# Two residual layers on one core: how the group carries of a sorted prefix sum reach the gathered rows

## The chip, the cores and the metric

One core of a Trainium2 chip runs the whole program. The metric is the device time in microseconds of one execution; the median of a few executions is given. A profile of one execution, with every instruction and transfer, stands beside it.

## What is computed

For each of 32 batches `x[b]` is a 512 x 1024 matrix (channels by nodes), and there are two layers, each with a residual and a layer normalization over the 1024 nodes. Cut to what matters:

```python
def _L0_gnn_ref(x, wq, wk, wm, bm):
    q = jnp.einsum('c,bcn->bn', wq, x)
    k = jnp.einsum('c,bcn->bn', wk, x)
    scores = q[:, None, :] + k[:, :, None]
    scores = jnp.where(scores > 0, scores, NEG_SLOPE * scores)
    att = jax.nn.softmax(scores, axis=-1)
    agg = jnp.einsum('bcn,bmn->bcm', x, att)
    out = jnp.einsum('oc,bcm->bom', wm, agg) + bm[None, :, None]
    return jax.nn.relu(out)

def _L1_gnn_ref(x, support, kernel, bias):      # support = kernel = adj
    W = support * kernel
    return jnp.einsum('bnf,nm->bmf', x, W) + bias

x = _layernorm(x + _L0_gnn_ref(x, wq, wk, adj, bm), axis=-1)
x = _layernorm(x + _L1_gnn_ref(x, adj, adj, bias), axis=-1)
```

Everything is float32. Layer 0's attention has scores that are a sum of one number of the row and one of the column, through a leaky ReLU. So the kernel does not form the 1024 x 1024 matrix. It sorts the columns by `q`. For a row with key `k`, the columns above a threshold have weight exp(q+k) and those below it exp(0.01 (q+k)). Each row is then a mix of two sums over sorted columns: one over all ranks from one side, one over all ranks from the other, both cut at that row's rank.

## The kernel before

**The stages of a batch**, with the short names that the order of the work uses. `ld` loads x (2 MB, four buffers in the pool `xp`). `pa pc co cc ro rc` make q and k. `rk` (VectorE) counts each column's rank among q, `ct` (ScalarE) counts for each row how many q lie above its threshold; `re` and `ce` turn them into row numbers `to` and `of`. `z` (TensorE) multiplies x by adj in eight blocks of 128 nodes, `zc` (ScalarE) copies each block to `zt`, and `sc` (GpSimd) scatters its 128 rows of 514 numbers to `sorted_z` in DRAM, at the ranks. `sl` (SyncE) loads `sorted_z` back, so that partition p holds the eight ranks 8p to 8p+7.

**The sums.** `se` makes the two exponentials, `u` (VectorE) the running sums over the eight ranks of each partition from one side, `d` those from the other. A sum over whole partitions, the carry, is missing in each. `cu` and `cd` (TensorE) make it by a product with a triangular matrix (`before` or `behind`) from the partition's totals, `uc` and `dc` (ScalarE) copy it out of PSUM. Then VectorE adds the carry to all ranks of the partition: `tu` (two parts, L405), `td` (two parts, L405), and `te` (L414) for the last row. `tw` (two parts, L422, SyncE) writes the table, 1024 rows of 2 x 514 numbers, to DRAM, and `tl` (L425) its last row.

**The mix.** `g` (GpSimd, L432) gathers eight times 128 rows of the table to `got`, by `of`. `mw` makes weights for four of the eight parts, `ms` (ScalarE) and `mx` (VectorE) mix the two halves of each row, `t` (TensorE) transposes to PSUM, `r` (VectorE) adds the residual, `s0` (ScalarE) sums squares. Layer 0's root is taken in one step when all four parts of `s0` are done: `rt` (ScalarE, square root, L500) and `rce` (VectorE, reciprocal, L504). `n0` (ScalarE) scales.

**Layer 1.** One level of a Strassen-Winograd product: `t1` to `t4` on VectorE, `U V Z Y 11 12 21` on TensorE, copies and sums on ScalarE and VectorE, then `s1`, `r1` (GpSimd), `n`, and the store `st`. Its operands `T3` and `T4` stand in `zt`, the buffer that `zc` fills and `sc` reads.

**Buffers.** The tile `tab`, which receives the loaded ranks and holds both running sums until `tw` has read them, has one buffer, and so has `got`. `zt` is one buffer too. `sorted_z` and `table` have two each in DRAM.

**What sets the order.** The order is written out: three strings of words, `head`, `loop` and `tail`, are read word by word and each word issues one step for one batch. Every engine and every queue works off its own instructions strictly in that order. `loop` covers one batch's worth of all steps on five batches in different stages (in a word such as `g.-2.3` the first number is the batch, counted from the loop's base, the second the part). In the kernel before it runs for 14 bases after a head of 11 batches; the tail drains the rest. Since GpSimd's queue is in order too, a gather whose table has not landed holds up every scatter and root behind it.

Of the kernel before, what the change touches and what calls it, by code (L numbers as in the profile page):

```python
# [41 lines left out]
P = 128  # L43
# [6 lines left out]
def adj_resnorm_kernel(  # L50
# [49 lines left out]
    room = one.tile([P, NT, 2 * ZR], F32, tag="tab", name="bias_in")[0:6, :, 0:H]  # L100
    for h in range(2):
# [7 lines left out]
    before = const.tile([P, P], F32, name="before")  # L109
    nc.vector.memset(before, 1.0)  # L110
    nc.gpsimd.affine_select(
        before, before, pattern=[[1, P]], compare_op=ALU.is_gt, fill=0.0, base=0,
# [23 lines left out]
    zero = one.tile([P, ZR], F32, tag="carry", name="zero")[0:1, :]  # L136
    nc.vector.memset(zero, 0.0)
    sorted_z = [dr.tile([N, ZR], F32, name=f"sorted_z_{i}") for i in range(2)]
    table = [dr.tile([N + 1, 2 * ZR], F32, name=f"table_{i}") for i in range(2)]
    for t in table:  # L140
        nc.scalar.dma_start(out=t[N : N + 1, ZR:], in_=zero)
    spare = const.tile([1, 1], F32, name="spare")
# [145 lines left out]
    def count_end(b):  # L288
        s = st[b]
        s.of = s4.tile([P, NT], U32, tag="of", name=f"of_{b}")  # L290
        nc.vector.tensor_scalar(s.of, s.sign, 0.5, N / 2, ALU.mult, ALU.add)
        s.bd = s4.tile([P, 2, NT], F32, tag="bd", name=f"bd_{b}")
        nc.vector.tensor_scalar(s.bd[:, 0, :], s.k, s.top, 0.0, ALU.add, ALU.min)
        nc.vector.tensor_scalar(s.bd[:, 1, :], s.k, s.top, 0.0, ALU.add, ALU.max)
# [37 lines left out]
    def sums_load(b, h):  # L332


        s = st[b]
        if h == 0:
            apart(f"ranks {b}", s.scatters)
            s.tab = one.tile([P, NT, 2 * ZR], F32, tag="tab", name=f"tab_{b}")
            s.zs = s.tab[:, :, ZR : 2 * ZR]
            s.ac = sp.tile([P, 2, NT], F32, tag="ac", name=f"ac_{b}")  # L340
        rows = sorted_z[b % 2].rearrange("(p j) c -> p j c", j=NT)
        at = slice(h * NT // 2, (h + 1) * NT // 2)
        nc.sync.dma_start(out=s.zs[:, at, :], in_=rows[:, at, :])
# [30 lines left out]
    def carry(b, m, v):  # L374
# [3 lines left out]
        for h in range(2):  # L378
            t = p1.tile([P, C], F32, tag="m", name=f"carry_ps_{b}_{h}_{m is before}")[:, 0:half]
# [9 lines left out]
    def carry_up(b):  # L389
        st[b].cup = carry(b, before, st[b].end)  # L390

    def carry_up_copy(b):
        carry_copy(st[b].cup, st[b].tab[:, 0, 0:ZR])

    def carry_down(b):
        st[b].cdown = carry(b, behind, st[b].zs[:, 0, :])
# [5 lines left out]
    def spread_carry(v, c):  # L402
        n = v.shape[1]
        c = c[:, 0:D].rearrange("p (o c) -> p o c", o=1).broadcast_to([P, n, D])
        nc.vector.tensor_tensor(v, v, c, ALU.add)  # L405

    def table_up(b, h):
        lo, hi = ((1, 4), (4, 8))[h]
        spread_carry(st[b].tab[:, lo:hi, 0:D], st[b].tab[:, 0, 0:ZR])

    def table_up_end(b):

        s, on = st[b], slice(96, P)
        nc.vector.tensor_tensor(s.end[on, 0:D], s.end[on, 0:D], s.tab[on, 0, 0:D], ALU.add)  # L414

    def table_down(b, h):
        spread_carry(st[b].zs[:, 4 * h : 4 * h + 4, 0:D], st[b].carry)

    def table_write(b, h):
        rows = table[b % 2][0:N, :].rearrange("(p j) c -> p j c", j=NT)  # L420
        at = slice(4 * h, 4 * h + 4)
        nc.sync.dma_start(out=rows[:, at, :], in_=st[b].tab[:, at, :])  # L422

    def table_last(b):
        nc.sync.dma_start(out=table[b % 2][N : N + 1, 0:ZR], in_=st[b].end[P - 1 : P, :])  # L425


    def gather(b, j):
        s = st[b]
        if j == 0:  # L430
# [3 lines left out]
            in_offset=bass.IndirectOffsetOnAxis(ap=s.of[:, j : j + 1], axis=0),  # L434
        )
# [62 lines left out]
    def root0(b):  # L498
            v = st[b].v0
            nc.scalar.activation(v[1], v[1], AF.Sqrt, scale=1.0 / N**3, bias=eps)  # L500

    def root0_end(b):
            v = st[b].v0
            nc.vector.reciprocal(v[1], v[1])  # L504
    
# [129 lines left out]
    def store(b, m):  # L635
# [10 lines left out]
        "cd": carry_down, "dc": carry_down_copy, "tu": table_up, "te": table_up_end,  # L646
        "td": table_down, "tw": table_write, "tl": table_last, "g": gather, "mw": mix_weights,
        "ms": mix_scale, "mx": mix, "t": turn, "r": residual, "s0": spread0, "rt": root0, "rce": root0_end,
# [5 lines left out]
    pool_ops = ("sc", "g", "r1")  # L654
# [10 lines left out]
    bias.0 ld.1 ld.2 ld.3 z.0.0 z.0.1 pa.0 z.0.2 pc.0 zc.0.0 zc.0.1 co.0 zc.0.2 pa.1 cc.0 ro.0  # L665
    pc.1 z.0.3 rc.0 rk.0.0 ct.0.5 ct.0.2 rk.0.1 z.0.5 ct.0.3 rk.0.6 zc.0.3 rk.0.4 ct.0.7 z.0.4
    rk.0.5 ct.0.1 rk.0.7 rk.0.2 z.0.6 zc.0.4 zc.0.5 rk.0.3 ct.0.0 oq.0 re.0 sc.0.4 z.0.7 zc.0.6
    sc.0.1 ct.0.6 sc.0.5 ct.0.4 sc.0.3 co.1 zc.0.7 z.1.0 cc.1 sc.0.6 sc.0.2 sc.0.0 ro.1 z.1.6
    sc.0.7 rc.1 ce.0 ct.1.0 rk.1.1 zc.1.0 rk.1.3 z.1.2 zc.1.6 sl.0.0 ct.1.7 sl.0.1 oq.1 rk.1.0
    rk.1.2 z.1.1 zc.1.2 rk.1.7 ct.1.1 rk.1.4 we.0 rk.1.6 z.1.5 se.0.0 ct.1.6 u.0.0 u.0.1 ct.1.2  # L670
    u.0.2 se.0.1 pa.3 ct.1.5 u.0.3 u.0.4 ct.1.4 z.1.7 u.0.5 zc.1.5 ct.1.3 u.0.6 u.0.7 zc.1.1
    pc.3 rk.1.5 z.1.4 zc.1.7 d.0.7 d.0.6 ce.1 d.0.5 z.1.3 zc.1.4 re.1 d.0.4 sc.1.7 d.0.3 sc.1.0
    d.0.2 sc.1.5 co.3 d.0.1 zc.1.3 cu.0 cc.3 d.0.0 sc.1.3 ro.3 uc.0 cd.0 sc.1.6 te.0 tu.0.1 pa.2
    sc.1.1 sc.1.2 z.2.0 tu.0.0 pc.2 dc.0 sc.1.4 td.0.0 z.2.2 rc.3 tw.0.0 td.0.1 ct.3.3 ct.3.0
    co.2 z.2.5 rk.3.4 tw.0.1 zc.2.0 tl.0 we.1 rk.3.0 ct.3.7 zc.2.2 rk.3.3 z.2.3 zc.2.5 ct.3.4
    rk.3.6 ct.3.1 rk.3.1 ct.3.6 z.2.6 rk.3.7 zc.2.3 cc.2 ct.3.2 rk.3.2 sl.1.0 g.0.0 ct.3.5
    sl.1.1 rk.3.5 ro.2 g.0.1 zc.2.6 z.2.1 rc.2 g.0.2 rk.2.0 ct.2.7 g.0.3 ct.2.4 g.0.5 rk.2.3
    z.2.4 g.0.4 rk.2.2 se.1.0 ct.2.3 g.0.7 rk.2.1 z.2.7 g.0.6 zc.2.4 rk.2.7 zc.2.1 ce.3 re.3
    rk.2.4 se.1.1 z.3.0 rk.2.6 zc.2.7 ct.2.0 rk.2.5 ct.2.5 mw.0.0 z.3.1 u.1.0 ms.0.3 re.2 oq.2
    ms.0.0 u.1.1 sc.2.3 ms.0.1 u.1.2 ct.2.6 sc.2.5 mx.0.0 u.1.3 z.3.4 ms.0.2 sc.2.2 mx.0.3  # L680
    mw.0.1 sc.2.0 mx.0.2 ms.0.5 sc.2.6 mx.0.1 ms.0.6 z.3.2 mx.0.5 ms.0.7 sc.2.1 mx.0.6 ms.0.4
    mx.0.7 ct.2.2 sc.2.4 mx.0.4 u.1.4 sc.2.7 t.0.3 u.1.5 t.0.1 r.0.3 r.0.1 t.0.0 s0.0.3 u.1.6
    zc.3.4 t.0.2 zc.3.0 r.0.0 zc.3.1 z.3.5 s0.0.1 u.1.7 s0.0.0 r.0.2 d.1.7 s0.0.2 oq.3 cu.1
    d.1.6 sc.3.1 rt.0 d.1.5 d.1.4 zc.3.2 d.1.3 uc.1 z.3.3 sc.3.2 rce.0 zc.3.5 d.1.2 n0.0.0
    sc.3.0 d.1.1 n0.0.1 d.1.0 n0.0.2 tu.1.0 cd.1 zc.3.3 U.0.0 dc.1 t1.0 sc.3.3 n0.0.3 td.1.0
    11.0.0 td.1.1 tw.1.0 Z.0.0 11.0.1 tu.1.1 Zc.0.0 Uc.0.0 ct.2.1 U.0.1 t2.0 tw.1.1 te.1 V.0.0
    t3.0 tl.1 ce.2 12.0.0 Vc.0.0 Uc.0.1 V.0.1 up.0.0 Y.0.0 Vc.0.1 s1.0.0 sl.2.0 Z.0.1 lr.0.0
    we.2 sl.2.1 r1.0.0 t4.0 Y.0.1 Zc.0.1 g.1.0 12.0.1 lr.0.1 g.1.1 se.2.0 21.0.0 u.2.0 g.1.2
    u.2.1 g.1.3 21.0.1 u.2.2 up.0.1 se.2.1 g.1.7 ll.0.0 z.3.6 ld.4 u.2.3 s1.0.1 u.2.4 we.3
    r1.0.1 ls.0.0 u.2.5 s1.0.2 u.2.6 ll.0.1 u.2.7 r1.0.2 cu.2 d.2.7 ls.0.1 d.2.6 z.3.7 uc.2  # L690
    mw.1.0 zc.3.6 te.2 g.1.4 s1.0.3 d.2.5 sc.3.6 n.0.0 tu.2.1 pa.4 g.1.5 ms.1.3 ms.1.2 tu.2.0
    g.1.6 ms.1.1 z.4.5 pc.4 zc.3.7 sc.3.4 n.0.2 d.2.4 mx.1.1 sc.3.5 ms.1.0 d.2.3 n.0.1 sc.3.7
    mx.1.2 co.4 z.4.4 d.2.2 st.0.1 r1.0.3 mw.1.1 mx.1.0 ms.1.7 d.2.1 ms.1.5 cc.4 ms.1.6 d.2.0
    ro.4 zc.4.5 mx.1.5 ms.1.4 cd.2 mx.1.7 n.0.3 mx.1.4 z.4.0 zc.4.4 rc.4 st.0.3 dc.2 tl.2 st.0.0
    mx.1.6 st.0.2 ct.4.0 mx.1.3 td.2.0 ct.4.1 t.1.3 t.1.1 ct.4.5 r.1.3 z.4.1 tw.2.0 ct.4.4 r.1.1
    zc.4.0 td.2.1 s0.1.1 t.1.0 ct.4.2 t.1.2 r.1.0 tw.2.1 s0.1.3 z.4.6 oq.4 r.1.2 s0.1.0 rk.4.1
    ct.4.3 z.4.3 rk.4.2 s0.1.2 rk.4.0 zc.4.1 rt.1 z.4.7 g.2.0 sl.3.0 zc.4.3 rce.1 rk.4.7 sl.3.1
    n0.1.2 g.2.1 rk.4.6 n0.1.0 g.2.4 n0.1.1 rk.4.4 z.4.2 g.2.2 zc.4.6 rk.4.5 n0.1.3 g.2.3 t1.1
    ct.4.6 g.2.7 U.1.1 rk.4.3 zc.4.2 se.3.0 g.2.6 t2.1 11.1.1 g.2.5 Uc.1.1 u.3.0 ct.4.7 u.3.1
    U.1.0 re.4 u.3.2 sc.4.3 se.3.1 u.3.3 11.1.0 sc.4.0 ce.4 u.3.4 sc.4.1 V.1.1 mw.2.0 u.3.5  # L700
    ms.2.2 sc.4.2 ms.2.0 Z.1.0 mx.2.2 ms.2.3 sc.4.4 zc.4.7 mx.2.3 Vc.1.1 Z.1.1 u.3.6 ms.2.1
    Uc.1.0 mw.2.1 u.3.7 V.1.0 ms.2.6 mx.2.1 Zc.1.0 mx.2.6 12.1.0 Vc.1.0 d.3.7 ms.2.5 t3.1 ms.2.4
    cu.3 up.1.0 ms.2.7 Zc.1.1 Y.1.0 t4.1 s1.1.0 Y.1.1 mx.2.7 uc.3 r1.1.0 lr.1.0 mx.2.4 21.1.0
# [259 lines left out]
```

## Time and profile before

| | |
|---|---|
| median of 3 runs | 2069.77 us (2066.95 to 2071.07) |
| the profiled execution | 2069.97 us, of which the span from first to last instruction is 2068.1 us |
| mean granted TensorE clock | 0.989 |
| busy | TensorE 2005.4 us, VectorE 1686.9, ScalarE 1494.8, GpSimd 848.7 |
| moved by DMA | 541.04 MB, mean 262 GB/s |

A row of the groups gives line, engine, operation, output and input, count, then busy time and mean duration of one, then the idle time of the engine before it and what ended that idle time. A row of a table by windows gives the stretch, its length, then for TensorE, its weight loads, VectorE, ScalarE and GpSimd the busy microseconds with the number of instructions, then the granted clock, the mean busy share of the core's 16 DMA engines, and GB/s. Queue q0 carries GpSimd's transfers, q1 those of SyncE.

### The profile page before, as it was taken

To read this page: it belongs to the slowest core of one execution; us is meant where nothing else is said; L and a number is where in the kernel's file an instruction comes from. 1 tells how busy PE (TensorE), PEld (TensorE's weight loads), DVE (VectorE), ACT (ScalarE), POOL (GpSimd) and SP (SyncE) were. 2 spreads that over 40 slices of the span, in tenths; PEclk is the share of its full clock that TensorE was granted. 3 is DMA by queue.
4 is the path that set the end of the run, shared out by engine and by line. 5 is a ranking of instruction groups with operands and counts; after the bars stand their busy time and mean duration, and the time that the engine had idled before them with its cause. 6 is when DMAs were issued, how large, how long until landed. Compare 5 with 4: busy or idle time off the path is not lost.

```text
span 2068.1 us, 22068 instructions
## 1 busy us (share of the span) xinstructions
PE 2005.4 (97%) x6609; PEld 958.9 (46%) x6609; DVE 1686.9 (82%) x2778; ACT 1494.8 (72%) x2560; POOL 848.7 (41%) x1088
## 2 busy tenths in 40 slices
PE   8999999999999999999999999999999999999976
PEld 4444444444444444544444444444544444444432
DVE  5988888887788888888888888888888888788663
ACT  3567777776777777777787777787777787767666
POOL 4234443453443443443443443443443443444331
PEclk9999999999999999999999999999999999999988
DMA  5568767766677766677766677766677756677752
GB/s 224 199 241 324 286 231 285 311 231 237 247 301 294 291 245 270 246 286 295 296 245 269 246 285 295 287 256 264 250 281 296 301 212 272 240 295 271 275 204 81
DMA packets 137967, 541.04 MB, mean 262 GB/s; under 512 B 14404, under 2 KB 14416, under 8 KB 129656
## 3 DMA queue, kind: packets, MB, share of 16 engines
q1 hardware_dynamic: 80464, 337.47, 41.6%
q0 software_dynamic: 57344, 202.15, 25.3%
q8 instruction: 52, 0.85, 0.2%
q14 instruction: 67, 0.55, 0.1%
q10 hardware_dynamic: 40, 0.02, 0.0%
HBM read 270.29 MB, written 269.29 MB: 261 GB/s over the span
## 4 chain that ended last, share of the span: by engine, by line
PE 71%; DMA 7%; DVE 6%; POOL 3%; ACT 2%; issue 2%; SPq 0%; ACTq 0%; DVEq 0%; POOLq 0%
PE z_ps L310 30%; PE sum_ps L540 16%; PE pair_ps L540 8%; DMA got<-table,of 5%; PE agg_ps L482 5%; PE pair_ps L575 4%; POOL got L432 3%; PE qk_ps L221 2%; DMA table<-end 1%; DVE got L459 1%; PE carry_ps_False L380 1%; DVE tab L405 1%; PE q_tp L252 1%; PE carry_ps_True L380 1%; PE sum_ps L538 1%
## 5 line engine op out<-in xcount | busy, mean ns | idle before, releaser
L310 PE MATMUL z_ps<-adj_t,x 128*128 128x512 f32 x2048 | 908.7, 593 | 2.9 <-ACT zt L316 2.0
L310 PEld LDWEIGHTS z_ps<-adj_t,x 128*128 128x128 f32 x2048 | 382.8, 190 | 441.9 <-issue 430.6
L324 POOL DMA_INDIRECT sorted_z<-zt,to x256 | 327.0, 1277 | 423.7 <-ACT zt L316 323.1
L432 POOL DMA_INDIRECT got<-table,of x256 | 268.8, 1050 | 331.9 <-DVE junk_v L271 117.3
L271 DVE SCALAR_TENSOR_TENSOR junk_v<-qb,qkc,tie 128x1024 uint8<-128x1024 f32 x256 | 328.5, 1283 | 6.0
L284 ACT ACTIVATE junk_s<-qb,qkc 128x1024 bf16<-128x1024 f32 x256 | 294.2, 1149 | 28.8 <-DVE qb L261 20.5
L475 POOL TENSOR_SCALAR var<-var 128x1 f32<-128x1 f32 x128 | 63.4, 496 | 427.0 <-ACT junk L468 411.8
L454 ACT ACTIVATE got<-got,w 128x512 f32<-128x512 f32 x256 | 170.5, 716 | 80.7 <-DVE w L449 61.1
L459 DVE SCALAR_TENSOR_TENSOR got<-got,w 128x512 f32<-128x512 f32 x256 | 185.2, 748 | 40.6 <-ACT got L454 39.2
L316 ACT COPY zt<-z_ps 128x512 f32<-128x512 f32 x256 | 145.5, 580 | 82.5 <-PE z_ps L310 82.2
L490 DVE SCALAR_TENSOR_TENSOR x<-agg_ps,nbm,x 128x1024 f32<-128x1024 f32 x128 | 160.4, 1281 | 17.6 <-PE agg_ps L482 17.4
L372 DVE SCALAR_TENSOR_TENSOR tab<-tab,ac 128x513 f32<-128x513 f32 x224 | 168.7, 753 | 2.7
L405 DVE TENSOR_TENSOR tab<-tab,carry 128x2052 f32<-128x2052 f32 x64 | 146.3, 2291 | 20.7 <-ACT carry L387 20.7
L631 ACT ACTIVATE g<-g,nb,var 128x1024 f32<-128x1024 f32 x128 | 157.6, 1233 | 6.0 <-POOL nb L625 6.0
L468 ACT ACTIVATE junk<-g,tot 128x1024 bf16<-128x1024 f32 x128 | 146.5, 1145 | 19.6 <-DVE g L595 11.9
L468 ACT ACTIVATE junk<-x,tot 128x1024 bf16<-128x1024 f32 x128 | 146.8, 1147 | 18.9 <-DVE x L490 18.0
L540 PE MATMUL sum_ps<-x,adj 128*128 128x512 f32 x256 | 132.7, 642 | 18.9 <-ACT x L508 18.9
L362 DVE SCALAR_TENSOR_TENSOR tab<-tab,ac 128x514 f32<-128x514 f32 x192 | 144.6, 753 | 4.4 <-ACT ac L348 0.9
L482 PE MATMUL agg_ps<-ident,got 128*128 128x128 f32 x1024 | 131.2, 280 | 16.0 <-DVE got L459 8.3
L508 ACT ACTIVATE x<-x,var 128x1024 f32<-128x1024 f32 x128 | 138.3, 1146 | 1.4 <-DVE var L504 1.3
L482 PEld LDWEIGHTS agg_ps<-ident,got 128*128 128x128 f32 x1024 | 116.5, 144 | 48.6 <-issue 17.1
L405 DVE TENSOR_TENSOR tab<-tab 128x1539 f32<-128x1539 f32 (+1 forms) x64 | 129.4, 2025 | 0.8 <-ACT tab L387 0.7
(121 smaller groups left out, 2614.2 us busy)
## 6 DMA issues: line engine op xcount, KB each, us to landing
table<-tab SPq DMA_DIRECT2D x64, 2056.0 KB
tab<-sorted_z SPq DMA_DIRECT2D x64, 1028.0 KB
x<-in_x_dram SPq DMA_DIRECT2D x128, 512.0 KB
out_dram<-g SPq DMA_DIRECT2D x128, 512.0 KB
sorted_z<-zt,to POOLq DMA_INDIRECT x256
got<-table,of POOLq DMA_INDIRECT x256
adj_in<-in_adj_dram SPq DMA_DIRECT2D x1, 1024.0 KB
table<-end SPq DMA_DIRECT2D x32, 2.0 KB
```

The costliest lines, as they stand in the source:

```text
L271: nc.vector.scalar_tensor_tensor(junk, s.qb, s.q[:, j : j + 1], tie[:, at : at + N], ALU.subtract, ALU.is_gt, accum_out=s.rank[:, j : j + 1],)
L284: nc.scalar.activation(junk, s.qb, AF.Sign, bias=s.k[:, j : j + 1], accum_out=s.sign[:, j : j + 1])
L310: nc.tensor.matmul(s.z[j], xt[:, c, j * P : (j + 1) * P], adj_t[:, c, :], start=(c == 0), stop=(c == CT - 1),)
L324: nc.gpsimd.indirect_dma_start(out=sorted_z[b % 2][:, :], out_offset=bass.IndirectOffsetOnAxis(ap=s.to[:, j : j + 1], axis=0), in_=zt[:, j ...
L372: nc.vector.scalar_tensor_tensor(v, v, c, s.zs[:, j + 1, 0:D], ALU.mult, ALU.add)
L405: nc.vector.tensor_tensor(v, v, c, ALU.add)
L432: nc.gpsimd.indirect_dma_start(out=s.got[:, j, :], out_offset=None, in_=table[b % 2][:, :], in_offset=bass.IndirectOffsetOnAxis(ap=s.of[:, ...
L454: nc.scalar.activation(down, down, AF.Copy, scale=s.w[:, 1, j : j + 1])
L459: nc.vector.scalar_tensor_tensor(up, up, s.w[:, 0, j : j + 1], down, ALU.mult, ALU.add)
L468: nc.scalar.activation(junk, t, AF.Square, bias=v[0][:, i : i + 1], scale=-float(N), accum_out=v[1][:, i : i + 1],)
L482: nc.tensor.transpose(s.agg[o][:, j * P : (j + 1) * P], s.got[:, j, o * P : (o + 1) * P], ident)
L540: nc.tensor.matmul(ps, a[:, k, g * P : (g + 1) * P], v[:, k, :], start=False, stop=(k == 1), skip_group_check=first is None,)
```

## The change

The additions `tu`, `td`, `te` and the write `tl` are gone. The table is written with the sums inside each partition alone. The carries go to a small table in DRAM of their own (`carries`, 129 rows of 2 x 514 numbers, two buffers), by two new writes `cw` (SyncE). After each gather `g` of 128 table rows, a second indirect transfer `h` reads for each of these rows the row `of >> 3` of `carries` and adds it to what is in `got`. The triangular matrix for one side now includes its diagonal (`upto`), so that the carry up to and with partition p is written one row further. `tab` becomes one lasting tile, whose first column block stays zero. Layer 0's root is taken in two halves on GpSimd (a multiply-add, then a power of -0.5), each when two of the four parts of `s0` are done. The three strings of the order are written anew throughout; the new head covers 12 batches, the loop again 14 bases.

```diff
+    tab = const.tile([P, NT, 2 * ZR], F32, name="tab")
+    zs = tab[:, :, ZR : 2 * ZR]
...
-    before = const.tile([P, P], F32, name="before")
+    upto = const.tile([P, P], F32, name="upto")
...
+    carries = [dr.tile([P + 1, 2 * ZR], F32, name=f"carries_{i}") for i in range(2)]
...
+        s.part_of = s4.tile([P, NT], U32, tag="part_of", name=f"part_of_{b}")
+        nc.vector.tensor_scalar(s.part_of, s.of, 3, None, ALU.logical_shift_right)
...
-    def spread_carry(v, c):
-        n = v.shape[1]
-        c = c[:, 0:D].rearrange("p (o c) -> p o c", o=1).broadcast_to([P, n, D])
-        nc.vector.tensor_tensor(v, v, c, ALU.add)
-
-    def table_up(b, h):
-        lo, hi = ((1, 4), (4, 8))[h]
-        spread_carry(st[b].tab[:, lo:hi, 0:D], st[b].tab[:, 0, 0:ZR])
-
-    def table_up_end(b):
-
-        s, on = st[b], slice(96, P)
-        nc.vector.tensor_tensor(s.end[on, 0:D], s.end[on, 0:D], s.tab[on, 0, 0:D], ALU.add)
-
-    def table_down(b, h):
-        spread_carry(st[b].zs[:, 4 * h : 4 * h + 4, 0:D], st[b].carry)
+    def carry_write(b, h):
+
+        t = carries[b % 2]
+        if h == 0:
+            nc.sync.dma_start(out=t[1 : P + 1, 0:ZR], in_=st[b].end)
+        else:
+            nc.sync.dma_start(out=t[0:P, ZR : 2 * ZR], in_=st[b].carry)
...
-    def table_last(b):
-        nc.sync.dma_start(out=table[b % 2][N : N + 1, 0:ZR], in_=st[b].end[P - 1 : P, :])
...
+    def gather_carry(b, j):
+        s = st[b]
+        nc.gpsimd.indirect_dma_start(
+            out=s.got[:, j, :], out_offset=None, in_=carries[b % 2][:, :],
+            in_offset=bass.IndirectOffsetOnAxis(ap=s.part_of[:, j : j + 1], axis=0),
+            compute_op=ALU.add,
+        )
...
-    def root0(b):
-            v = st[b].v0
-            nc.scalar.activation(v[1], v[1], AF.Sqrt, scale=1.0 / N**3, bias=eps)
-
-    def root0_end(b):
-            v = st[b].v0
-            nc.vector.reciprocal(v[1], v[1])
-    
+    def root0(b, h):
+        root(st[b].v0, slice(2 * h, 2 * h + 2))
```

The words of GpSimd, of SyncE, and of the weights that wait for the gathers, in the order in which the loop issues them (words of the other steps left out):

```
loop before: g.-3.7 g.-3.5 r1.-4.0 mw.-3.0 ld.0 mw.-3.1 r1.-4.1 sc.-1.0 sc.-1.1 st.-4.1
  st.-4.0 r1.-4.3 sc.-1.2 r1.-4.2 sc.-1.3 st.-4.2 st.-4.3 sc.-1.4 sc.-1.5 tw.-2.0 tw.-2.1
  sc.-1.7 sc.-1.6 tl.-2 sl.-1.0 sl.-1.1 g.-2.0 g.-2.3 g.-2.1 g.-2.2 g.-2.4 g.-2.6
loop after:  cw.-3.1 rt.-4.1 sc.-2.6 g.-3.0 g.-3.7 g.-3.1 g.-3.6 g.-3.3 g.-3.4 g.-3.2 h.-3.0
  h.-3.4 h.-3.3 h.-3.2 sc.-2.7 h.-3.1 h.-3.7 sl.-2.0 r1.-4.0 sl.-2.1 mw.-3.0 g.-3.5 h.-3.6
  r1.-4.1 ld.0 h.-3.5 r1.-4.2 r1.-4.3 st.-4.2 st.-4.0 mw.-3.1 st.-4.1 sc.-1.0 sc.-1.1 sc.-1.3
  sc.-1.2 tw.-2.1 sc.-1.4 cw.-2.0 rt.-3.0 tw.-2.0 st.-4.3 sc.-1.5
```

## The prediction

> **What bounds the kernel now.** First the page: the busy shares and the DMA queues.
>
> ```profile
> span 2068.1 us, 22068 instructions
> PE 2005.4 (97%) x6609; PEld 958.9 (46%) x6609; DVE 1686.9 (82%) x2778; ACT 1494.8 (72%) x2560; POOL 848.7 (41%) x1088
> ...
> q1 hardware_dynamic: 80464, 337.47, 41.6%
> q0 software_dynamic: 57344, 202.15, 25.3%
> ```
>
> TensorE is busy 97%, but a share over the span says nothing of where the other 3% lies. So the second view is busy time by windows: head, middle, tail.
>
> ```profile
> 0.00:557.10 557.10, 532.96 (x1825) 255.56 (x1826) 455.43 (x762) 376.87 (x661) 234.79 (x294) 0.99 0.67 257
> 557.10:1671.30 1114.20, 1114.12 (x3707) 534.86 (x3706) 943.74 (x1549) 843.21 (x1443) 467.31 (x597) 1.00 0.69 273
> 1671.30:2068.10 396.80, 358.30 (x1080) 168.47 (x1078) 287.71 (x469) 274.76 (x459) 146.62 (x199) 0.95 0.62 237
> ```
>
> The middle is 18 batches of 61.90 us, and TensorE idles 0.08 us in 1114.2, at full clock. VectorE has 170 us to spare there. Nothing that leaves VectorE or ScalarE can shorten these 18 batches; the change touches TensorE's steps only in their order. All that can be won is 24.1 us of idle TensorE in the head and 38.5 us in the tail, and much of that is filling and draining.
>
> Third, what the change loads instead: the DMA engines. Windows of 2 us inside one batch of the middle:
>
> ```profile
> 1164.00:1166.00 2.00, 2.00 (x6) 0.95 (x5) 2.00 (x5) 1.48 (x4) 1.83 (x2) 1.00 0.01 4
> 1176.00:1178.00 2.00, 2.00 (x6) 0.81 (x6) 2.00 (x3) 1.56 (x3) 1.46 (x4) 1.00 0.00 0
> 1206.00:1208.00 2.00, 2.00 (x6) 0.81 (x5) 1.96 (x4) 1.98 (x5) 1.39 (x3) 1.00 1.05 410
> 1210.00:1212.00 2.00, 2.00 (x6) 0.95 (x5) 1.21 (x2) 1.66 (x6) 1.39 (x3) 1.00 1.06 417
> 1216.00:1218.00 2.00, 2.00 (x6) 0.94 (x5) 1.87 (x7) 0.56 (x2) 0.00 (x0) 1.00 1.03 406
> ```
>
> The last two columns are the DMA share and GB/s. The mean of 0.69 is made of stretches with nothing to move and of one, from the gathers on, that stands at 1.03 to 1.06 and 410 GB/s: the ceiling. Packets overlap slightly, so full is about 1.04.
>
> Fourth, groups of instructions by line, for the prices:
>
> ```profile
> L432 POOL DMA_INDIRECT got<-table,of x256 | 268.8, 1050 | 331.9 <-DVE junk_v L271 117.3 <-DMA table<-end 74.0 <-issue 69.8
> L405 DVE TENSOR_TENSOR tab<-tab,carry 128x2052 f32<-128x2052 f32 x64 | 146.3, 2291 | 20.7 <-ACT carry L387 20.7
> L405 DVE TENSOR_TENSOR tab<-tab 128x1539 f32<-128x1539 f32 (+1 forms) x64 | 129.4, 2025 | 0.8 <-ACT tab L387 0.7
> L476 POOL TENSOR_TENSOR var<-var,power 128x1 f32<-128x1 f32 x128 | 100.3, 783 | 10.7
> L500 ACT ACT_TABLE_LOAD x31 | 39.8, 1283 | 0.5
> ```
>
> Last the timeline of the tail, TensorE and then VectorE:
>
> ```profile
> 1988.49 3.78 PE L540 MATMUL sum_ps<-x,adj 128*128 128x512 f32 x4 [9.54 <-ACT x L508]
> 2016.87 2.00 PE L482 MATMUL agg_ps<-ident,got 128*128 128x128 f32 x16
> ...
> 2003.94 0.17 DVE L445 TENSOR_TENSOR w<-bd,got 128x8 f32<-128x8 f32 x1 [9.77 <-DMA got<-table,of]
> ```
>
> TensorE waits 9.54 us for layer 0's scaling, and the last batch's weights wait 9.77 us for its gathers.
>
> **The change part by part.** *Off VectorE*, per batch: L405 (146.3 + 129.4) / 32 = 8.62 us, L414 0.69, L504 0.18; on comes one shift of eight numbers, 0.17 as the row of `of`. Net 9.3 of about 52.4 busy in 61.9 us. *Off ScalarE*: the square root, 0.30, and the table loads that it forces (39.8 + 32.1 + 6.4 over the three lines, 2.4 per batch). In the middle both gains are worth nothing: these engines already wait for TensorE.
>
> *On GpSimd*, per batch: eight more indirect issues at 1.05 (gather row) to 1.28 (scatter row), 8.4 to 10.2 us, and two roots at 0.50 + 0.78, 2.6 us. 25.9 becomes 37 to 39 of 61.9: room. But `h` must wait for its gather to land and for `cw`. Behind the first four `h` stands `sc.-2.7`, the last scatter of the next batch. `sl` needs that scatter, and so does everything after it (`se`, `u`, `d`, `tw`, the next gathers). Behind later `h` stand `r1` and so `n` and `st`, which have slack.
>
> *On SyncE*: two `cw` for one `tl`, some 0.24 us each to issue; free. `cw.-3.1` stands ahead of `sl`, which waits longer for the scatter anyway. `tw` no longer waits for `tu`, `td`.
>
> *On the DMA engines.* q0's price is 0.253 x 2068.1 / 202.15 = 2.59 us of all 16 engines per MB, q1's 0.416 x 2068.1 / 337.47 = 2.55. Per batch `cw` writes 0.53 MB: 1.3 us. `h` moves 8 x 128 x 4112 B = 4.21 MB: 10.9 us as a plain gather. An adding transfer stands nowhere in this trace. Below: 10.9, the gather's row, nothing hidden. It cannot be less, since the same bytes are fetched. Above: 21.8, twice that row, since what is in `got` has to be fetched too. I take 21.8, as `got` plus row is two operands through the engines that one gather keeps at their ceiling. Three times, 32.7, if the return trip also serializes, is the far end.
>
> A rule of the Trainium skill speaks against the change here. "Collectives: The Full Stack", section "The bandwidth ceiling: the fold count and why AG ≠ RS ≠ AR", says that the add itself costs nothing but needs two source reads on one ring, with 62.28 against 32.35 GB/s, 1.93 times, measured for collectives. By it `h` would be an estimated 21.0 us; no row here shows it.
>
> The sum per batch: 0.69 x 61.9 = 42.7 us now, plus 1.3, plus `h`. Plain: 54.9 (share 0.89). Doubled: 65.8, at a full rate of 1.04 an interval of 63.3 us, over TensorE's 61.9. Not divided by 1.04 it would be 65.8, and gaps, where the chain has nothing to move, come on top. I take 63.3, since the stretches now empty (1164, 1176) get work and the writes of the table start earlier. So +1.4 us on each of 18 batches: 25.
>
> *Head*: it ran at a DMA share of 0.67 with TensorE idle 24.1 us while pipes fill. There the gathers' landing is on the path. Doubled, I add the same 1.4 for some four batches with all stages running, 6; between -3 (lighter VectorE) and +12.
>
> *Tail*: the last batch's `tu`, `td`, `te`, `tl` go (table whole at 1986, gathers at 1993.4; after, the write can start some 8 us earlier, 1985). Eight gathers and eight adds then take 32.7 us instead of 10.9, landed near 2020 against about 2009: with mixing, `t` near 2027 against 2016.9 in the row. TensorE's work on batch 30, which now hides the chain, ends there: +10 at most. The earlier scaling (no table load, halves) gives back about 3 of the two waits on L508, and VectorE's relief as much again: +4. Plain: landed near 2009 as now, so the gain of 6 stays.
>
> Total: 25 + 6 + 4 = 35 us. Span 2068.1 + 35 = 2103; the profiled execution is 1.9 over its span and 0.2 over the median: 2105.
>
> **The rivals.** *The adds cost no more than gathers, and TensorE keeps the middle.* For it: 54.9 of 61.9 leaves 7 us free, VectorE has over 18 us to catch up in, GpSimd 23. Against it: eight waits for landings in one queue. Then the middle stays at 61.90 and only head and tail move: -3 and -6, 2061; from 2048 (a third of the idle in head and tail regained) to 2077 (a longer fill through `h`). This is the other side: it decides when `h` stays under (61.9 x 1.04 - 44.0) = 20.4 us per batch, 1.9 plain gathers.
>
> *GpSimd's queue becomes the cycle.* `tab` has one buffer: `sl`, sums, `tw`, landing, then gathers, four `h`, `sc.-2.7`, `sl` again. At three times the price, 42.7 + 1.3 + 32.7 = 76.7, or 73.8 at 1.04: +11.9 x 18 = 214, 2280. With doubled adds late by one landing each it lies at +3 to +6 per batch: 2130 to 2180. For it: the gathers' first landing already blocks GpSimd for 74.0 us (row L432). Against: between `sl` and `se` the loop has three parts of layer 1 and a `z` on TensorE (12 instructions of about 0.47 us and 8 of 0.44 by the busy times of their lines, 9 us) that such a delay can use up first.
>
> *The change does less than it says* can be shut out: the order listing shows TensorE's steps equal in number, `tu`, `td`, `te` gone and 256 `h` there.
>
> **How the numbers follow.** Doubled adds, DMA at its ceiling, +15 to +75: 0.47. Plain adds: 0.37. The slow cycle, over +75: 0.16. Predicted is the first, 2105. The range leaves out the best tenth of the second and the worse half of the third: 2052 to 2190. Runs of this kernel lie 0.2% apart, about 4 us, and less cannot be told from no change. Faster by more than that: three quarters of the plain case, 0.28. Same: 0.09. Slower: 0.63.
>
> **What would show it.** In the windows of the middle: the interval of a batch (61.9 or 63 and more), TensorE idle, and DMA share near 1.0 in mean. In the groups: VectorE about 300 us less busy, no table loads on ScalarE, GpSimd near 1200. In the queues: q0 at 25.3% plus 17% (plain) or 34% (doubled). In the waits: VectorE's `mw` on `got`, TensorE's `t` on `mx`. I am wrong if q0's growth is doubled and the middle still runs at 61.9, or if the span grows with a DMA share below 0.95 there.

## The result, and the profile after

The kernel after takes 2351.72 us (median of 4 runs, 2347.39 to 2357.34), the kernel before on the same chip 2070.28: a ratio of 1.1355 [1.1338, 1.1373]. It is slower, as forecast, but by 281 us instead of 35, and 162 us above the upper end of the range. The profiled execution has a span of 2345.4 us against 2068.1: 277.3 more to explain.

The page of the kernel after, its busy shares, its DMA queues, and the shares of the chain that ended last:

```profile
span 2345.4 us, 22526 instructions
PE 2092.9 (89%) x6609; PEld 977.1 (42%) x6609; DVE 1403.5 (60%) x2618; ACT 1409.8 (60%) x2467; POOL 1275.8 (54%) x1430
...
q0 software_dynamic: 94208, 336.90, 55.0%
q1 hardware_dynamic: 89616, 354.25, 38.3%
...
DMA 38%; PE 17%; POOL 13%; DVE 10%; issue 10%; ACT 7%; SPq 0%; POOLq 0%; ACTq 0%; another core or an unknown queue 0%; DVEq 0%
```

VectorE lost 283 us and ScalarE 85, GpSimd gained 427, and the chain now runs through DMA (38%) more than through TensorE (17%). Busy time by windows, same columns as before:

```profile
0.00:557.10 557.10, 486.40 (x1571) 230.19 (x1575) 332.45 (x634) 312.83 (x563) 296.23 (x331) 0.95 0.90 287
557.10:1671.30 1114.20, 1023.32 (x3264) 474.69 (x3257) 687.31 (x1283) 694.99 (x1218) 633.98 (x695) 0.97 0.97 307
1671.30:2345.40 674.10, 583.22 (x1779) 272.23 (x1777) 383.75 (x703) 402.01 (x688) 345.60 (x406) 0.93 0.90 282
```

TensorE idles 90.9 us in the middle stretch, where it idled 0.08. (The stretch now holds some 16 batches instead of 18.) TensorE also needs longer for the same 6609 products: 2092.9 us against 2005.4, at a granted clock of 0.97 in this stretch against 1.00. The chain runs through TensorE for 17% of the span, so an estimated 17 us of the 277.3 (0.17 x 2345.4 x 87.5 / 2092.9) can be this; no run separates it. The DMA share went from 0.69 to 0.97, but the rate only from 273 to 307 GB/s, far from the 410 of a full stretch in the kernel before: busy engines that move less.

The time is lost everywhere, not in one stage. With a batch's start taken as its first product for q and k on TensorE, batch 13 (counted from 0) starts 99.1 us later than before; from there to the start of batch 25 it takes 842.4 us instead of 742.8 (an interval of 70.2 us instead of 61.9), from there to the start of batch 31 60.1 us more, and what follows 18.5 more: 99.1 + 99.6 + 60.1 + 18.5 = 277.3.

Groups by line: the two indirect transfers to `got`.

```profile
L438 POOL DMA_INDIRECT got<-carries,part_of x256 | 424.0, 1656 | 229.3 <-DMA got<-table,of 168.4
L431 POOL DMA_INDIRECT got<-table,of x256 | 281.3, 1099 | 111.8 <-issue 66.5
```

An `h` takes GpSimd 1656 ns to issue, half as much again as a `g`, and GpSimd waits 168.4 us in front of `h` for `g` to land. Five rows of the waits, by who waited for whom (total, times, longest):

```profile
POOL var L482 <- ACT junk L475: 376.1, 111, 21.4
POOL sorted_z L335 <- ACT zt L327: 220.5, 114, 11.2
POOL got L438 <- DMA got<-table,of: 168.4, 57, 8.9
ACT ac L359 <- DMA tab<-sorted_z: 143.8, 52, 7.0
DVE w L452 <- DMA got<-carries,part_of: 126.5, 36, 11.8
```

The first two are long, but GpSimd waited as long for ScalarE in the kernel before (411.8 us ahead of layer 1's roots, 323.1 ahead of scatters), where the middle ran at 61.9. The fourth is the one to keep in mind: ScalarE's `se` waits for the ranks that `sl` loads back to `tab`, a transfer that the change did not touch.

The chain in order of time shows why. One batch of the middle, from the writing of one table to the gathers from the next and a little beyond (start, length, what; `...` stands for pieces left out):

```profile
1198.29 9.33 DMA table<-tab
...
1208.50 3.72 DMA got<-table,of
...
1217.97 1.64 POOL got L438
...
1227.29 8.47 DMA sorted_z<-zt,to
...
1236.28 16.65 DMA tab<-sorted_z
...
1274.14 0.72 POOL var L483
...
1275.36 0.88 POOL sorted_z L335
...
1276.98 4.56 DMA got<-table,of
...
1300.12 7.67 DMA got<-carries,part_of
```

This is a loop: table landed, seven gathers issued, four `h` issued, behind them the next batch's last scatter (`sc.-2.7`), its landing, the load of the ranks, the running sums, the write of the table, the next gathers. It took 68.5 us here. The load of the ranks is released by the scatter's landing and not by the one buffer of `tab`: the load is issued 28.6 us after the table before it has landed (mean of batches 12 to 24).

Two other ways run beside this loop. At its end this chain goes through layer 0's root and a scatter on GpSimd; the table landed at 1276.18, just ahead of the gathers, which on the mean start 0.8 us after the table's landing. And in the next batch the chain leaves the loop at 1300.12 with the landing of an add, for which VectorE's `mw` waits. So a move of words that shortens one way can leave another in place. The same stretch by windows:

```profile
1208.50:1227.30 18.80, 18.80 (x51) 8.24 (x50) 13.02 (x22) 12.96 (x24) 13.64 (x12) 1.00 0.89 250
1227.30:1235.80 8.50, 6.94 (x17) 2.76 (x15) 1.03 (x3) 1.14 (x2) 7.17 (x8) 1.00 1.03 213
1235.80:1253.00 17.20, 15.68 (x32) 6.35 (x32) 10.66 (x28) 9.19 (x20) 8.32 (x11) 0.90 1.04 298
1262.50:1277.00 14.50, 14.14 (x57) 8.30 (x56) 8.58 (x14) 10.75 (x18) 5.84 (x10) 1.00 1.00 405
```

While the scatter lands and the ranks load, the engines are full (1.03 and 1.04) at 213 and 298 GB/s: the adds, which GpSimd issues from 1218 to 1245, are in the way. Later in the same batch a full share moves 405.

### The profile page after: what moved, and what is told of

It is laid out like the page before. It is cut to its first block, busy times and chain, and to the rows that moved or that the text cites. A ratio compares the mean times of both kernels' runs of the same rounds, so it can differ in the third digit from the quotient of the medians.

```text
span 2345.4 us, 22526 instructions
## 1 busy us (share of the span) xinstructions
PE 2092.9 (89%) x6609; PEld 977.1 (42%) x6609; DVE 1403.5 (60%) x2618; ACT 1409.8 (60%) x2467; POOL 1275.8 (54%) x1430
## 4 chain that ended last, share of the span: by engine, by line
DMA 38%; PE 17%; POOL 13%; DVE 10%; issue 10%; ACT 7%; SPq 0%; POOLq 0%; ACTq 0%; another core or an unknown queue 0%; DVEq 0%
DMA tab<-sorted_z 15%; DMA sorted_z<-zt,to 8%; PE z_ps L321 8%; POOL got L438 7%; DMA got<-table,of 6%; POOL got L431 5%; DMA got<-carries,part_of 4%; DMA table<-tab 4%; DVE got L466 3%; PE agg_ps L489 3%; DVE tab L383 3%; PE sum_ps L542 2%; DVE x L497 2%; ACT g L633 2%; ACT got L461 1%
## 5 line engine op out<-in xcount | busy, mean ns | idle before, releaser
L321 PE MATMUL z_ps<-adj_t,x 128*128 128x512 f32 x2048 | 926.2, 604 | 42.7 <-ACT zt L327 20.1
L321 PEld LDWEIGHTS z_ps<-adj_t,x 128*128 128x128 f32 x2048 | 391.9, 195 | 523.9 <-issue 456.5
L438 POOL DMA_INDIRECT got<-carries,part_of x256 | 424.0, 1656 | 229.3 <-DMA got<-table,of 168.4
L335 POOL DMA_INDIRECT sorted_z<-zt,to x256 | 297.1, 1160 | 306.3 <-ACT zt L327 220.5
L431 POOL DMA_INDIRECT got<-table,of x256 | 281.3, 1099 | 111.8 <-issue 66.5
L293 ACT ACTIVATE junk_s<-qb,qkc 128x1024 bf16<-128x1024 f32 x256 | 294.4, 1150 | 20.3 <-DVE qb L270 17.7
L482 POOL TENSOR_SCALAR var<-var 128x1 f32<-128x1 f32 (+1 forms) x192 | 68.9, 359 | 382.4 <-ACT junk L475 376.1
L542 PE MATMUL sum_ps<-zt,adj 128*128 128x512 f32 x256 | 149.8, 718 | 85.0 <-DVE g L603 85.0
L489 PE MATMUL agg_ps<-ident,got 128*128 128x128 f32 x1024 | 151.4, 291 | 47.2 <-DVE got L466 32.1
L497 DVE SCALAR_TENSOR_TENSOR x<-agg_ps,nbm,x 128x1024 f32<-128x1024 f32 x128 | 162.9, 1279 | 30.1 <-PE agg_ps L489 26.9
L597 DVE SCALAR_TENSOR_TENSOR g<-pair_ps,g 128x1024 f32<-128x1024 f32 x64 | 78.2, 1222 | 118.6 <-ACT g L587 74.6
L483 POOL TENSOR_TENSOR var<-var,power 128x1 f32<-128x1 f32 (+1 forms) x192 | 136.1, 709 | 16.1
```

The source lines that it names most:

```text
L293: nc.scalar.activation(junk, s.qb, AF.Sign, bias=s.k[:, j : j + 1], accum_out=s.sign[:, j : j + 1])
L321: nc.tensor.matmul(s.z[j], xt[:, c, j * P : (j + 1) * P], adj_t[:, c, :], start=(c == 0), stop=(c == CT - 1),)
L335: nc.gpsimd.indirect_dma_start(out=sorted_z[b % 2][:, :], out_offset=bass.IndirectOffsetOnAxis(ap=s.to[:, j : j + 1], axis=0), in_=zt[:, j ...
L431: nc.gpsimd.indirect_dma_start(out=s.got[:, j, :], out_offset=None, in_=table[b % 2][:, :], in_offset=bass.IndirectOffsetOnAxis(ap=s.of[:, ...
L438: nc.gpsimd.indirect_dma_start(out=s.got[:, j, :], out_offset=None, in_=carries[b % 2][:, :], in_offset=bass.IndirectOffsetOnAxis(ap=s.par ...
L489: nc.tensor.transpose(s.agg[o][:, j * P : (j + 1) * P], s.got[:, j, o * P : (o + 1) * P], ident)
```

## Experiments

Three theories stood at the start. *Totals* (T): the DMA engines have more than 61.9 us of work per batch, and the interval is that work. *The small table*: many rows of the 129-row table are read again and again, and that is what is slow. *A chain*: the new waits in series set the interval. A fourth came up, that the new order is slow whatever the transfers cost. All figures below are medians; a ratio is to the kernel before on the same chip, with its 95% interval; the interval of a batch is the mean over twelve batches, from the start of q and k in batch 13 to that in batch 25. In the pieces of the order shown below, words of other steps are left out.

### What an adding transfer costs by itself

**m1_alone**: the transfers with nothing beside them.

```diff
+    def gt(b, j): got_row(b, j, table[0], st[b].of)
+    def gc(b, j): got_row(b, j, carries[0], st[b].part_of)
+    def ht(b, j): got_row(b, j, table[0], st[b].of, compute_op=ALU.add)
+    alone: gt x48, gc x48, h x48, ht x48, then gt.0.0 x6, h.0.0 x6 (each waiting for the one before)
```

> Only batch 0's table is made; then 48 transfers of 128 rows each, back to back, in four blocks: plain from the big table, plain from the small one, adding from the small one, adding from the big one; then six plain and six adding ones on one part, each waiting for the one before to land. The output is not the reference's. The add itself is dear: about 1.3 us per plain transfer from either table, 2.7 to 3.0 per adding one from either. Rival, the small table's 129 rows are read too often: the plain block from the small table is as slow as the adding one from it, and adding from the big table costs about 1.3.

Windows of this run: plain gathers from the table, plain from the small table, adding from the small table, adding from the table.

```profile
110.00:150.00 40.00, 0.00 (x0) 0.00 (x0) 0.00 (x0) 0.00 (x0) 30.25 (x33) 0.50 1.03 411
170.00:200.00 30.00, 0.00 (x0) 0.00 (x0) 0.00 (x0) 0.00 (x0) 22.68 (x25) 0.50 1.03 412
260.00:320.00 60.00, 0.00 (x0) 0.00 (x0) 0.00 (x0) 0.00 (x0) 36.52 (x24) 0.50 1.06 210
350.00:400.00 50.00, 0.00 (x0) 0.00 (x0) 0.00 (x0) 0.00 (x0) 30.81 (x20) 0.50 1.07 210
```

Plain, one follows another after 1.24 us; adding, after 60 / 24 = 2.50. That is 2.0 times (1.96 by the rates), at a full share in both, and it makes no difference which table is read. The small table fell as a theory. Where each waits for the one before, plain ones stand 4.6 us apart and adding ones 6.6. Eight adds are 20 us of all engines, close to the 21.8 of the prediction.

### How the interval goes with the adds

**e1_plain**: `h` overwrites instead of adding. **e2_four**: four of the eight add.

```diff
 e1_plain
-            compute_op=ALU.add,
 e2_four
+        add = dict(compute_op=ALU.add) if j in (0, 2, 5, 6) else {}
-            compute_op=ALU.add,
+            **add,
```

> The second transfer h stays in its place with its waits and its bytes, but overwrites instead of adding (the carries' sums are lost). DMA engines as the bound: 42.7 + 1.3 + 10.9 = 54.9 us per batch lie under TensorE's 61.9 again, 2055 to 2090 us. Rival, GpSimd's queue (eight waits for landings, sixteen issues) as the bound: above 2200. Rival, the small table's rows: still about 2350.

> Parts 0, 2, 5, 6 add, the other four overwrite. DMA engines as the bound: 42.7 + 1.2 + 4 x 3.0 + 4 x 1.36 = 61.4 us per batch, at the share of 0.97 that the changed kernel reaches 63.2, so +1.4 on some 31 batches: 2095 to 2135. Rival, GpSimd's queue: about halfway, 2200 or more.

**e5_none**: `h` is left out altogether, GpSimd writes one number in its place, and `mw` takes its weights without the gathered ones, so that it waits for no landing.

```diff
-        nc.gpsimd.indirect_dma_start(out=s.got[:, j, :], ..., compute_op=ALU.add)
+        nc.gpsimd.memset(spare, 0.0)
-            nc.vector.tensor_tensor(w, bd, ones, ALU.mult)
+            nc.vector.tensor_tensor(w, bd, bd, ALU.mult)
```

> The changed kernel without any h (a tiny memset in its place; the weights take the bound instead of the gathered ones, so the carries are left out and the mix is not the reference's). What the new order costs by itself. Both theories: interval 61.9, 2055 to 2085 us. Rival, that the new order is slow whatever the transfers: above 2150.

| | time, us | ratio | interval, us |
|---|---|---|---|
| no `h` (e5_none) | 2052.89 | 0.9913 [0.9894, 0.9931] | 61.9 |
| eight plain (e1_plain) | 2118.07 | 1.0214 [1.0188, 1.0241] | 63.6 |
| four add (e2_four) | 2223.02 | 1.0740 [1.0704, 1.0776] | 66.4 |
| eight add (after) | 2351.72 | 1.1355 [1.1338, 1.1373] | 70.2 |

The order of e5_none is that of the kernel after, so the order is not slow by itself, and all that the change takes off VectorE and ScalarE, together with the new order, is worth 18 us if the gathering of carries costs nothing. The middle windows of e5_none and e1_plain:

```profile
557.10:1671.30 1114.20, 1114.20 (x3709) 533.41 (x3708) 780.45 (x1455) 793.60 (x1386) 484.27 (x791) 1.00 0.75 281
```

```profile
557.10:1671.30 1114.20, 1094.84 (x3646) 522.11 (x3645) 762.51 (x1419) 770.50 (x1347) 596.39 (x771) 1.00 0.91 339
```

Without `h` TensorE has no idle time. With plain `h` it idles 19 us although the DMA share is 0.91, well under full: already here it is no matter of totals. The second four adds cost more than the first four (3.8 us of interval against 2.8). TensorE's granted clock in the middle is 1.00 in e2_four and 0.97 in the kernel after, so part of the second step may be the clock.

### Is it the total of the transfers?

**e3_stores**: half of the output is not stored, which takes 1 MB, about 2.7 us of all engines, out of each batch.

```diff
     def store(b, m):
+        if m >= 2 and b < B - 1:
+            return
```

> The changed kernel with two of the four output blocks of each batch but the last not stored: 1.05 MB per batch less on the DMA engines, 2.7 us, and nothing less for GpSimd, VectorE or TensorE. DMA engines as the bound: 31 x 2.7 = 83 us less, 2255 to 2285. Rival, GpSimd's queue or another chain: within 15 us of 2352.

2349.43 us, 1.1335 [1.1316, 1.1353], interval 70.2. Its middle window:

```profile
557.10:1671.30 1114.20, 1021.35 (x3274) 473.70 (x3273) 687.65 (x1283) 695.51 (x1218) 631.79 (x697) 0.97 0.94 292
```

The share fell from 0.97 to 0.94 and the interval stayed. Totals fell as a theory: less to move, no faster.

### Where in the loop the adds cost

These are read from the traces of the same runs: starts on the engines, mean over batches 12 to 24, from a batch's first gather to the issue of the next batch's last scatter; from there to the last use of the loaded ranks in `se`; from there to the next first gather. The three add up to the interval (within 0.2) by construction; what tells is which of them grows.

| us | gathers to last scatter | scatter to ranks in use | sums, table, to next gathers |
|---|---|---|---|
| e1_plain | 17.7 | 18.8 | 27.1 |
| e2_four | 18.3 | 22.7 | 25.3 |
| after | 19.5 | 25.6 | 25.0 |
| e3_stores | 19.4 | 25.6 | 25.1 |
| e16_load | 19.9 | 25.5 | 30.5 |
| e10_both_plain | 9.9 | 27.0 | 26.6 |
| e9_both | 10.3 | 32.6 | 30.1 |
| e15_free_plain | 10.6 | 28.3 | 29.5 |
| e12_free | 10.6 | 36.4 | 29.1 |

Between e1_plain and the kernel after, 6.5 us apart, the middle stage grows by 6.8, the first by 1.8, the third shrinks by 2.1. The chain of e1_plain has the same two transfers in one of its batches:

```profile
1240.34 5.52 DMA sorted_z<-zt,to
1245.92 9.32 DMA tab<-sorted_z
```

5.52 and 9.32 us (13.60 in the batch before), where the kernel after has 8.47 and 16.65. The scatter and the ranks' load move the same bytes in both; in the kernel after they share the engines with adds queued ahead of and beside them. The means over the same batches, first from the scatter's issue to the issue of the load, then from there to the landing of the load's second half, grow with the adds while the bytes stay: 4.8 and 8.2 us without `h` (e5_none), 5.7 and 12.8 beside plain ones, 6.6 and 15.9 beside four adds, 8.3 and 17.1 beside eight. From plain to eight adds they grow by 2.6 and 4.3 us, which is the growth of the middle stage. This also fits e3_stores: a store stands behind `sl` in SyncE's queue, so it never held the load up.

### Attempts to break the loop by moving words

**e4_scatter**: the last scatter goes ahead of the four `h`.

```diff
-    g.-3.2 h.-3.0 h.-3.4 h.-3.3 h.-3.2 sc.-2.7 h.-3.1
+    g.-3.2 sc.-2.7 h.-3.0 h.-3.4 h.-3.3 h.-3.2 h.-3.1
```

> The changed kernel, all adds kept; in loop and tail the last scatter of the next batch (sc.-2.7) is issued ahead of the first h instead of behind four. Theory now: the bound is a cycle through the one buffer tab (table landed, gathers, four adds, this scatter, its landing, load of the ranks, sums, table written), not the DMA engines' total. Then some 9 us of issue and waits and part of the scatter's 8.5 us of landing leave the cycle; what else waits takes over, so the interval falls from 70.2 to between 62 and 66 us, 2130 to 2240 us. Rival, the total of DMA time: the same packets, 2335 to 2360. A third: GpSimd's total of work, also unchanged.

2391.56 us, 1.1552 [1.1526, 1.1579], interval 72.5: worse. The first stage fell to 9.7 us, the second rose to 34.0. The scatter lands early, and the ranks then load while gathers and adds go through: the load takes 26.1 us instead of 17.1. VectorE's `mw`, which stands in front of the running sums, now waits for the adds, 346.0 us in all against 126.5:

```profile
DVE w L452 <- DMA got<-carries,part_of: 346.0, 53, 13.6
```

**e8_mix** takes the other side of that: `mw.-3.0` with its `ms` and `mx` goes behind the ranks' first sums. **e9_both** has both moves, **e10_both_plain** the same with overwriting `h`, **e11_both_st** e9_both without half of the stores.

```diff
-    sl.-2.1 mw.-3.0 g.-3.5 ms.-3.2 h.-3.6 ... u.-2.1 r1.-4.2 u.-2.2
+    sl.-2.1 g.-3.5 h.-3.6 ... u.-2.1 r1.-4.2 mw.-3.0 ms.-3.2 ms.-3.0 ... mx.-3.0 u.-2.2
```

> The changed kernel; in loop and tail the first half of the mix (mw.-3.0 with its four ms and mx) is issued behind layer 1's last additions (lr, up, ls) instead of ahead of them. Theory now: two chains of about 70 us each run through the adds. One goes by the scatter behind four adds, the load and the sums to the table. The other goes by the landing of the first four adds to mw, which holds VectorE's queue and so lr, TensorE's next products, the transposes, the residual and the table. This takes the second away and leaves the first: 70.2 falls by 1 to 2 us, 2300 to 2350. Rival, the total of DMA time: 2340 to 2360.

> As e8_mix, and sc.-2.7 ahead of the adds as in e4_scatter: both chains are freed, with the same packets. Theory of the two chains: 64 to 67 us per batch, by the DMA engines' total of 42.7 + 1.2 + 8 x 2.5 = 64, 2130 to 2230. Rivals that see no chain: 2340 to 2400.

> As e9_both with plain second transfers that overwrite (the sums of the carries are lost). If the two chains also made e1_plain's 63.6 us, the middle is back at TensorE's 61.9: 2050 to 2085. Rival: 63.6 had another cause, 2105 to 2125.

> As e9_both with two of the four output blocks of each batch but the last not stored, 2.7 us of DMA time per batch less. If the DMA engines' total bounds e9_both, this is 40 to 85 us below it. If a chain still does, within 15 us of it.

e8_mix 2411.11 us, 1.1625 [1.1603, 1.1646]; e9_both 2411.14, 1.1624 [1.1592, 1.1655]; e10_both_plain 2133.95, 1.0285 [1.0263, 1.0307]; e11_both_st 2414.28, 1.1643 [1.1606, 1.1679]. None helps. With both moves the adds cost 72.9 - 63.6 = 9.3 us of interval, more than in the order of the change: the load of the ranks takes 17.9 us beside plain transfers and 26.5 beside adds. Fewer stores again change nothing.

**e12_free** puts the scatter ahead, gathers part 5 with the others (so that `h.-3.5` finds it landed), and issues `d` and `tw` ahead of `mw.-3.1`; **e13_sums** has the last of these alone, **e14_pair** the second alone, **e15_free_plain** is e12_free with overwriting `h`.

```diff
 e13_sums
-    mw.-3.1 st.-4.1 sc.-1.0 u.-2.7 ms.-3.7 sc.-1.1 d.-2.7 d.-2.6 ...
+    u.-2.7 d.-2.7 d.-2.6 d.-2.5 d.-2.4 tw.-2.1 ... d.-2.0 tw.-2.0 mw.-3.1 st.-4.1 ...
 e14_pair
-    g.-3.2 h.-3.0 ... mw.-3.0 g.-3.5 ms.-3.2
+    g.-3.2 g.-3.5 h.-3.0 ... mw.-3.0 ms.-3.2
```

> The changed kernel, all adds kept, three moves of order in loop and tail: sc.-2.7 ahead of the adds; g.-3.5 with the other seven gathers, so that h.-3.5 need not wait for it at the end; the sums d of the next batch and its table writes ahead of mw.-3.1 on VectorE. Theory now: one loop of waits sets the interval, table landed, gathers, adds, the late pair g.5 and h.5, mw.1, which stands ahead of d on VectorE, d, table written. This breaks it; left is the DMA total of 64: 64 to 67 us per batch, 2130 to 2230. Rival, that adds are slower beside other transfers and the total really is 70: 2330 to 2400.

> The last of the three moves of e12_free alone. The loop of waits over mw.1 is broken; the way over the scatter behind four adds, the load of the ranks and the sums remains, about 66 to 68 us: 2230 to 2310. Rival: no change, 2335 to 2360.

> The second move alone: g.-3.5 with the other gathers. It takes the serial pair off the end, but the scatter comes one transfer later; 68 to 70 us per batch, 2300 to 2350. Rival: no change.

> As e12_free with plain second transfers that overwrite (the carries' sums are lost): DMA 54 us per batch, no loop of waits: 61.9 and 2050 to 2080. Rival: 63.5 as in e1_plain and e10_both_plain, 2110 to 2130.

e12_free 2462.84 us, 1.1878 [1.1858, 1.1899], interval 76.2; e13_sums 2480.97, 1.1967 [1.1946, 1.1987], 77.2; e15_free_plain 2206.02, 1.0664 [1.0635, 1.0693], 68.3, so that this order is slow with plain transfers too; e14_pair 2332.9, 1.1257 [1.1239, 1.1276], 69.2. Only e14_pair gains, 1 us of interval: the load of the ranks takes 15.4 us instead of 17.1, now that the gather of part 5 is not issued beside it. With e12_free and e15_free_plain the adds again cost 8 us, and again in the middle stage (28.3 to 36.4; the load 18.6 and 27.1).

Why e13_sums is slow can be read from its trace. Its sums are sooner: the table is whole 18.8 us after the last `se` instead of 24.2. But the first gather is issued 12.1 us after the table has landed, where it was 0.8 in the kernel after. Ahead of it in GpSimd's queue stand scatters and the roots of layer 0, and these wait for ScalarE. e12_free and e15_free_plain, which have the same move, show 10.2 and 10.7 us.

**e16_load** issues the load of x later, behind `u.-2.6`; **e17_pair_load** adds e14_pair's move.

```diff
-    mx.-3.1 ld.0 mx.-3.0 h.-3.5 u.-2.0 ... u.-2.6 st.-4.0
+    mx.-3.1 mx.-3.0 h.-3.5 u.-2.0 ... u.-2.6 ld.0 st.-4.0
```

> The changed kernel with all its work; only the load of x (2.1 MB, 5.3 us of DMA time) is issued later in loop and tail, behind the first store instead of right behind the load of the ranks. If the 70.2 us are a loop of waits whose stretch from the gathers to the last add is full of transfers, traffic moved out of that stretch shortens it, although the total stays: 66 to 69 us, 2250 to 2330. If the total of DMA time or GpSimd sets it: 2335 to 2360. If the load then only meets the table's write, which is on the loop too: no change or worse.

> e14_pair with the load of x moved as in e16_load. The two act on the same stretch: below e14_pair by about what e16_load is below the changed kernel, 2230 to 2310. If the load meets the table's write: 2330 or more.

e16_load 2449.74 us, 1.1847 [1.1810, 1.1883], interval 75.7; e17_pair_load 2430.84, 1.1733 [1.1689, 1.1777], 75.9. Taking 2 MB away from the time of the ranks' load left the middle stage at 25.5, and the third grew by 5.5, where the load now meets the write of the table, whose first half lands 13.4 us after its issue instead of 7.4. (By q1's 2.55 us per MB, 2.1 MB are about 5.3.) Both are transfers of SyncE's queue. Right behind the ranks' load the load of x costs the loop nothing (25.6 with it, 25.5 without), ahead of the table's write it costs what it takes. The adds, from GpSimd's queue, lengthen the ranks' load beside which they run.

### The other parts of the change, put into the kernel before

**e6_root**: layer 0's root in halves on GpSimd, all else as before. **e7_last**: also the last row of the table made and written early.

```diff
 e6_root
-    def root0(b):         (ScalarE, square root; then root0_end, VectorE, reciprocal)
+    def root0(b, h):
+        root(st[b].v0, slice(2 * h, 2 * h + 2))
 e7_last: te right behind tu.1, tl as soon as te and tw.0 are issued
```

> The kernel before with the second part of the change alone: layer 0's root in two halves on GpSimd, each put right after the second of its sums of squares. The middle is TensorE's, so nothing there; in the tail the scaling comes 1 to 2 us sooner for three batches and the table loads go: 2062 to 2070. Rival: GpSimd now waits for these sums ahead of scatters, 2075 to 2090.

> As e6_root, and the last row of the table (te, tl) right after the other additions and the first table write instead of some 10 us later. Middle unchanged, in head and tail the gathers start 1 to 3 us sooner: 2056 to 2068. Rival: te delays the start of layer 1 on VectorE, no gain over e6_root.

e6_root 2075.37 us, 1.0024 [1.0013, 1.0036]; e7_last 2092.48, 1.0103 [1.0084, 1.0122]; both keep the interval of 61.9. The root's halves cost 5 us where the prediction gave a gain of some 3 us in the tail, and moving the last row costs 17 us more; why is not shown.

## Why the prediction was off

**Right: the price of the add.** Of the bounds 10.9 and 21.8 us per batch the upper was taken, "two operands through the engines". Alone it is 20.0, 2.0 times plain. In the kernel q0 grew from 0.253 x 2068.1 = 523 us to 0.550 x 2345.4 = 1290: 767 / 32 = 24.0 us per batch. In e1_plain it is 0.448 x 2120.0 = 950, so a plain `h` costs 13.3 there. The Trainium skill ("Collectives: The Full Stack", section "The bandwidth ceiling: the fold count and why AG ≠ RS ≠ AR") gives 1.93 times, measured for collectives. The 2.0 of m1_alone (1.96 by the rates) agrees with it outside of them, and its price, an estimated 21.0 us instead of 21.8, would not have led to another forecast.

**Right: what leaves and comes on the engines.** VectorE 283 us less for about 300; ScalarE 85 less for 86 (2.7 x 32); no gain from either in the middle. GpSimd 1276 us for about 1200: an adding issue takes 1.66 us and was put between 1.05 and 1.28, the plain rows.

**Nearly right: the sum of DMA time.** 65.8 us per batch predicted; 0.97 x 70.2 = 68.1 measured.

**The step that failed** is the next one: "Doubled: 65.8, at a full rate of 1.04 an interval of 63.3 us", with "gaps, where the chain has nothing to move, come on top" priced at nothing, "since the stretches now empty (1164, 1176) get work". It took the sum as the bound and let the new 20 us spread to wherever the engines were idle. They do not spread: the adds are issued at one place, from the gathers into the load of the next ranks, and the loop of waits passes through exactly that place. The dose shows it: no `h` 61.9, eight plain 63.6, then 2.8 and 3.8 us of interval for each four adds, and nothing at all for 2.7 us of stores. The term was +1.4 us per batch and measured +8.3. That the change came out slower, as forecast, is therefore partly luck: the price of the add was right, but the bound that turned it into time does not hold, as the plain case below shows.

**The same step made the head and tail too small.** +6 and +4 stood there for what measured 99.1 us until batch 13 starts and 78.6 after batch 25 starts. The loop runs in all batches that have a table to wait for, so the cost is nearly that of all batches and not of 18; 8.3 x 32 would be 266 of the 277.

**The rivals.** The plain case was to give 2061, with the middle at 61.90 while `h` stays under 20.4 us per batch. e1_plain has 13.3 and takes 2118.07, with 63.6: the bound by totals was wrong in this case as well, and of the runs with the new order only the one without `h` (e5_none) keeps 61.9. The third rival named the loop that is seen: "`sl`, sums, `tw`, landing, then gathers, four `h`, `sc.-2.7`, `sl` again". It was given 0.16, and its price for doubled adds, "late by one landing each", was +3 to +6 us per batch, since it counted waits on GpSimd. It also gave the one buffer of `tab` as the reason for the loop, where the load is issued 28.6 us after the table before has landed. The larger part is elsewhere: the first stage, GpSimd's, grew by 1.8 us over plain, the scatter's landing and the ranks' load by 6.8. Its slack ("three parts of layer 1 and a `z` on TensorE") did not absorb that. The sign of being wrong, that "the span grows with a DMA share below 0.95", did not appear in the kernel after, whose share is 0.97: a share near 1 fits both a bound by totals and this loop. Only e3_stores tells them apart, with 0.94 and the same span.

**What stays open.** That the adds lengthen the scatter and the ranks' load is read from stages of traces that differ in the adds alone, in three orders (e1_plain to after, e10_both_plain to e9_both, e15_free_plain to e12_free: +6.8, +5.6, +8.1). That an order exists in which this load runs free of them is not shown: each attempt but one was slower, and of the forecasts for moves that were to shorten the loop only that of e14_pair was met. How much of the loss TensorE's lower clock adds is not separated. A second buffer for `tab` or `got` was not tried; for `tab` the 28.6 us speak against a gain. No version with all of its work beat the kernel before.

## What to carry to other kernels

Price an added transfer at the place where it is issued: look at which transfer of the kernel's loop is in flight then or comes behind it, and add the new time to that one; an idle stretch elsewhere in the batch did not take it up here. A DMA share near 1 does not prove that the total is the bound: take away a transfer that nothing waits for and see whether the interval moves. Before spending DMA time to relieve an engine, see whether that engine is waited for: here VectorE had 170 us to spare in the middle, and all of its relief, with the new order, was worth 18 us.

## What the runs showed of the hardware

By itself (m1_alone) an adding indirect transfer moves 210 GB/s where a plain one moves 411, both at a full DMA share (1.06 and 1.03), so a full share does not tell the rate; it also takes GpSimd 1.54 us to issue against 0.94, and 2.0 us longer from one landing to the next (6.6 against 4.6). Reading a table of 129 rows over and over cost nothing: 412 GB/s against 411. In the kernel, transfers of GpSimd's queue lengthen a load of SyncE's queue that runs beside them: 8.2 us without second gathers, 12.8 beside plain ones, 17.1 beside adding ones.
